# Bias of Exp and Square as a number in the instruction, in a four-layer graph kernel

## The chip, the cores and the metric

The kernel runs on one core of a Trainium2 chip. A core has five engines with a queue of instructions each: PE multiplies matrices into PSUM, DVE and POOL do elementwise work and reductions, ACT evaluates functions such as Exp, Square and Sigmoid, and SP issues DMAs. The engines run beside one another and wait on semaphores. The metric is the device time of one execution in microseconds (us), lower is better.

## The reference

Four graph layers run one after the other on x (4096 nodes, 64 features) with one adjacency matrix (4096 x 4096, zeros and ones). Each is followed by `x = layernorm(x + layer(x))`.

- Layer 0: neighbours' mean (`adj @ x`), a linear layer, relu, row normalization.
- Layers 1 and 3, the hyperbolic attention layers: for every pair of nodes i, j a weight `sigmoid(left_i + right_j + b) * adj_ij` times a curve of the pair's distance, then a sum over j:

```python
adj_att = sigmoid(left[:, None] + right[None, :] + b_att[0]) * adj
x_local = logmap(x[:, None, :], x[None, :, :], c)
support_t = einsum('ij,ijd->id', adj_att, x_local)
return proj(expmap(x, support_t, c), c)
```

- Layer 2: of each row's neighbours the last counts 1, the one before it 1/2, then 1/4 and so on, by a running count of the row's ones:

```python
pos = rank - (deg - k)
w = mask * where(pos > 0, 0.5 ** (k - pos), 0.0)
out = w @ (x @ weight) + bias
```

## The kernel before

The nodes are cut into 32 blocks of 128 (`BLOCKS`, taken from the last to the first) and into 4 groups of 1024 columns (`GROUPS`, also from the last). Each layer passes over all groups, and in each group over 16 loads of adjacency (`load`, L698), 1 MB each and two blocks wide, issued on SP into six buffers. Row work on a finished group (normalizing, the next layer's operands) is written as Python generators, of which `tick` advances a few steps at each block, so that it is issued among the next group's pair work.

**Attention (layers 1 and 3, function `attend`).** For one block j and 1024 columns:
- PE forms `z` in PSUM, three matmuls for each half of 512 columns (L1059 adds the adjacency, L1062 and L1065 the pair's distance). `z` has three buffers.
- ACT makes `sig`, the Sigmoid of `left_b` with a bias column of `right` (L1074). This bias differs by row and stays a pointer.
- ACT makes `sq[:, k]`, the Square of `z` (L1077). Its bias is the tile `turn`, one number in each of 128 partitions, all equal.
- DVE multiplies the cut-off `z` by `sig` into `t[:, k]` (L1080).

After two blocks DVE combines `sq` and `t` in one instruction over 2048 columns (L1082). `sq` has two buffers, `t` and `sig` three. PE sums `t` over the blocks into `acc` (L1037), two pairs of blocks late. There are 128 such pairs, 64 in each attention layer.

**Layer 2 (`wide_pass` for the first two groups together, `narrow_pass` for the third and fourth).** PE adds to a running count in `z` for each block (L1569, function `count`); ACT turns the count into the weight by an Exp (L1576, function `weights_of`), whose bias is the tile `at_edge`, again the same number in all partitions; PE multiplies the weights with `halves` (L1581, `add_up`). The count stays in the same PSUM tile from block to block, so that PE can add the next block only when Exp has read the last one. An Exp reads 1024 columns in the wide pass and 512 in the narrow ones.

**Order.** Layers 0 and 2 are issued under `tc.manual_schedule(engines=FIXED)`, which keeps PE and ACT in the order written. Attention is not: there the framework's scheduler orders each engine's instructions, with row work tied behind pair work by `mark`. DVE and POOL are ordered by the scheduler throughout. A tile that is written and read gets its semaphore waits from the framework.

The two constants are written once at the start:

```python
turn = num(keep, "turn", 1)
V.memset(turn, ROOT + OFF)
at_edge = num(keep, "at_edge", 1)
V.memset(at_edge, -(OFF_EDGE + CUT) * LN2)
```

A copy without a function (`nc.scalar.copy`) also runs on ACT, among others `sums` from `acc` (L1088), `top` and `low` (L1439, L1441), `left_b` (L1021) and the operands of row work (L947). Its casts of `ys` and `yd` are L899 to L901. Row work also has a Square of `u` without bias (L1134), a Tanh without bias (L1164), and Ln with a bias of 1.0 given as a number (L950, L951).

Of the kernel before, what the change touches and what calls it, by code (L numbers as in the profile page):

```python
# [14 lines left out]
AF = mybir.ActivationFunctionType  # L15
# [28 lines left out]
ROOT = 1.3933509672239  # L44
OFF = 0.044942809516658
HIGH = 1.3261200051291
Z_TOP = 0.0655
UNIT = 2.0**16
MEAN_TOP = 1e-10

LN2 = 0.6931471805599453
OFF_EDGE = 255.0
CUT = 27.0
# [5 lines left out]
def gnn_stack_kernel(  # L59
# [15 lines left out]
    nc = tc.nc  # L75
    V = nc.vector
# [11 lines left out]
    for src, at in ((b0, 0), (b2, D), (b_att1, 2 * D), (b_att3, 2 * D + 1), (r1, 2 * D + 2)):  # L88
        n = src.shape[0]
# [22 lines left out]
    def num(pool, name, n=NB):  # L112
        return pool.tile([P, n], F32, name=name)
# [455 lines left out]
    def stream(fits):  # L569

        with ExitStack() as st:

            def pool(name, bufs=1, **kw):
                return st.enter_context(tc.tile_pool(name=name, bufs=bufs, **kw))

            keep = pool("f_keep")
# [37 lines left out]
            def tick(n):  # L614
                for _ in range(n):
                    place[1] += 1
                    mark(False)
                    for queue in queues:
                        while queue and queue[0][1] <= place[1]:
                            wait = next(queue[0][0], None)  # L620
                            if wait is None:
                                queue.pop(0)
                                continue
                            queue[0][1] = place[1] + wait
                            if wait:
                                break
                    mark(True)

            def later(steps, second=False, wait=0):
                queues[second].append([steps, place[1] + wait])  # L630

            def in_turn(tag, *parts):
                for part in parts:
                    yield from (part or ())
                done.add(tag)
# [5 lines left out]
            def need(tag):  # L641
                while tag not in done:
                    assert queues[0] or queues[1], tag
                    tick(1)
# [51 lines left out]
            def load(s, g):  # L696
                a = loads.tile([P, 2, WW], F32, name="edges")
                nc.sync.dma_start(a, adj[s, :, 2 * g : 2 * g + 2, :])  # L698

                return a, a.rearrange("p b i -> p (b i)").bitcast(BF16)[:, 1::2]  # L700
# [79 lines left out]

            two_i = keep.tile([P, P], BF16, name="two_i")
            V.tensor_scalar(two_i, ident, 2.0 * UNIT, None, ALU.mult)
            turn = num(keep, "turn", 1)
            V.memset(turn, ROOT + OFF)


            centre = keep.tile([P, 2, D + 1], F32, name="centre")
# [209 lines left out]
            def in_order(one, behind):  # L997

                tc.add_manual_dep(
                    one, behind.name,  # L1000
                    mybir.DependencyInfo(
                        mybir.DependencyClass.NoSync, mybir.DependencyReason.DATA
                    ),
                    reason="order of issue",
                )

            def spread_left(s):

                left_bs[s] = lefts.tile([P, WW], F32, name="left_b")
                for h in range(2):  # L1010
                    yield from free()
                    t = take(F32, P, W)
                    for k in range(SB):
                        nb = s * WB + h * SB + k
                        nc.tensor.transpose(
                            t[:, k * P : (k + 1) * P],
                            left[:, nb : nb + 1].to_broadcast([P, P]),
                            ident,
                        )
                    yield near()  # L1020
                    nc.scalar.copy(left_bs[s][:, h * W : (h + 1) * W], t)  # L1021
                    held.pop()
                    yield 1

            def attend(layer, s, rate, then):

                left_b = left_bs[s]

                acc = ps.tile([P, W], F32, name="acc")
                lag = []  # L1030

                def add_up(g, t, behind=None):

                    for k in (1, 0):
                        j = 2 * g + k
                        for h in range(2):
                            it = nc.tensor.matmul(  # L1037
                                acc[h * D : (h + 1) * D, :], xe[:, j, :],
                                t[:, k, h * W : (h + 1) * W],
                                start=j == BLOCKS[0], stop=j == BLOCKS[-1],  # L1040
                            )
                            if behind is not None:
                                in_order(it.ins, behind.ins)

                for g in reversed(range(NB // 2)):
                    _, edge = load(s, g)
                    need((layer, 2 * g // WB))
                    if g == 4 and then is not None:
                        later(in_turn((layer, then, "left"), spread_left(then)), True)
                    for k in (1, 0):  # L1050
                        j = 2 * g + k
                        of = slice(j * P, (j + 1) * P)

                        zp = z_tile()
                        for h in range(2):
                            half = zp[:, h * W : (h + 1) * W]
                            to = slice(s * WW + h * W, s * WW + (h + 1) * W)
                            at = k * WW + h * W
                            nc.tensor.matmul(  # L1059
                                half, two_i, edge[:, at : at + W], start=True, stop=False  # L1060
                            )
                            nc.tensor.matmul(  # L1062
                                half, hi_lo[:, of], lo_hi[:, to], start=False, stop=False
                            )
                            last = nc.tensor.matmul(  # L1065
                                half, src[:, of], dst[:, to], start=False, stop=True
                            )
                        if k == 1:
                            if len(lag) == 2:
                                add_up(*lag.pop(0), last)  # L1070
                            sq = sb.tile([P, 2, WW], F32, name="sq")
                            t = sb.tile([P, 2, WW], F32, name="t", bufs=3)
                        sig = sb.tile([P, WW], F32, name="sig", bufs=3)
                        nc.scalar.activation(  # L1074
                            sig, left_b, AF.Sigmoid, bias=right[:, j : j + 1]
                        )
                        nc.scalar.activation(  # L1077
                            sq[:, k], zp, AF.Square, bias=turn, scale=-1.0 / UNIT
                        )
                        V.scalar_tensor_tensor(t[:, k], zp, 0.0, sig, ALU.max, ALU.mult)  # L1080
                        tick(rate)
                    V.scalar_tensor_tensor(t, sq, HIGH**2, t, ALU.add, ALU.mult)  # L1082
                    lag.append((g, t))
                    tick(rate)
                for args in lag:
                    add_up(*args)
                sums = row.tile([P, W], F32, name="sums", bufs=2)
                nc.scalar.copy(sums, acc)  # L1088
                return sums
# [200 lines left out]
            )  # L1290
            V.tensor_sub(enter, enter, edge_of)
            V.tensor_sub(pass_by, pass_by, enter)
            at_edge = num(keep, "at_edge", 1)
            V.memset(at_edge, -(OFF_EDGE + CUT) * LN2)


            w2_twice = keep.tile([P, D], F32, name="w2_twice")
# [157 lines left out]
            def z_tile():  # L1455
                return ps.tile([P, WW], F32, name="z", bufs=3)
# [116 lines left out]

            def weights_of(z, n, w):

                weighed[0] = nc.scalar.activation(w, z[:, :n], AF.Exp, bias=at_edge, scale=-LN2)  # L1576

            def add_up(acc, j, *ws):
                for part in range(2):
# [8 lines left out]
            weighed = [None]  # L1588
# [46 lines left out]
            sq = row.tile([P, D], F32, name="w_sq")  # L1635
# [16 lines left out]

    fits = const.tile([P, 1], F32, name="fits")
    stream(fits)

    n_fit = const.tile([1, 1], I32, name="n_fit")
# [54 lines left out]
```

## Time and profile before

| what | value |
|---|---|
| median of 3 runs | 1103.39 us (1102.56 to 1103.76) |
| profiled execution, its own time | 1103.6 us |
| its span, first to last instruction | 1101.8 us |
| mean granted PE clock | 0.966 |
| busy: PE, DVE, ACT, POOL | 997.7, 916.4, 795.1, 273.5 us |
| L1077, Square of attention | 256 instructions, 277.9 us |
| L1576, Exp of layer 2 | 128 of 512 columns, 81.3 us, and 64 of 1024 columns, 68.0 us |
| L1074, Sigmoid of attention | 256 instructions, 286.0 us |
| attention of layer 1 and of layer 3 | about 195 to 520 us and 750 to 1070 us |
| layer 2 | about 520 to 750 us |

A row of a group of instructions gives line, engine, operation, output<-inputs, shapes and count; after the first bar the busy time in us and the mean duration of one in ns; after the second the engine's idle time just before them, and what ended it. A row of the chain of waits in order of time gives start in us, length in us, and the work: the chain goes back from the last instruction, at each step to what released it or to the instruction before it on its engine. "issue" is time in which the engine waited for nothing that the profile shows, and a name with q is the engine's sequencer. Instructions that follow one another overlap in their records, so starts are a better measure of pace than durations.

### The profile page before, as it was taken

To read this page: it belongs to the slowest core of one execution; us is meant where nothing else is said; L and a number is where in the kernel's file an instruction comes from. 1 tells how busy PE (TensorE), PEld (TensorE's weight loads), DVE (VectorE), ACT (ScalarE), POOL (GpSimd) and SP (SyncE) were. 2 spreads that over 40 slices of the span, in tenths; PEclk is the share of its full clock that TensorE was granted. 3 is DMA by queue.
4 is the path that set the end of the run, shared out by engine and by line. 5 is a ranking of instruction groups with operands and counts; after the bars stand their busy time and mean duration, and the time that the engine had idled before them with its cause. 6 is when DMAs were issued, how large, how long until landed. Compare 5 with 4: busy or idle time off the path is not lost.

```text
span 1101.8 us, 13740 instructions
## 1 busy us (share of the span) xinstructions
PE 997.7 (91%) x4862; PEld 394.3 (36%) x4949; DVE 916.4 (83%) x1452; ACT 795.1 (72%) x886; POOL 273.5 (25%) x649
## 2 busy tenths in 40 slices
PE   4998997889999999998998998998899999999980
PEld 2454454333333333332333333322333333333320
DVE  6677976999999999999457395636999999999986
ACT  0003122979999999897676778989899999998950
POOL 0011210010053533625500010100001544346172
PEclk8999998889999999999998999999999999999995
DMA  9999999536666566655787988776556666666400
GB/s 358 378 411 388 369 421 382 189 122 223 214 244 211 195 234 214 222 198 184 271 304 280 366 298 277 273 261 229 191 192 217 241 228 202 238 222 228 163 1 23
DMA packets 38581, 271.63 MB, mean 247 GB/s; under 512 B 4710, under 2 KB 4710, under 8 KB 5734
## 3 DMA queue, kind: packets, MB, share of 16 engines
q1 hardware_dynamic: 37728, 270.03, 67.4%
q8 instruction: 41, 0.67, 0.2%
q10 hardware_dynamic: 774, 0.63, 0.2%
q14 instruction: 38, 0.31, 0.1%
HBM read 269.58 MB, written 1.05 MB: 246 GB/s over the span
## 4 chain that ended last, share of the span: by engine, by line
PE 56%; DVE 26%; ACT 8%; DMA 3%; POOL 3%; issue 3%; ACTq 0%; SPq 0%; POOLq 0%; DVEq 0%
PE acc L1037 15%; PE z L1569 9%; DVE t L1082 8%; PE z L1062 7%; PE z L1059 7%; PE z L1065 6%; DVE t L1080 6%; PE acc L1581 3%; PE acc L1414 3%; ACT sq L1077 3%; DMA edges<-in_adj_dram 3%; DVE junk L838 2%; ACT sq L1576 2%; PE z L1581 1%; POOL sq L869 1%
## 5 line engine op out<-in xcount | busy, mean ns | idle before, releaser
L1080 DVE SCALAR_TENSOR_TENSOR t<-z,sig 128x1024 f32<-128x1024 f32 x256 | 309.3, 1219 | 13.8 <-ACT sq L1077 7.5
L1077 ACT ACTIVATE sq<-z,turn 128x1024 f32<-128x1024 f32 x256 | 277.9, 1111 | 46.5 <-PE z L1065 19.4
L1082 DVE SCALAR_TENSOR_TENSOR t<-sq,t 128x2048 f32<-128x2048 f32 x128 | 297.4, 2324 | 0.5
L1074 ACT ACTIVATE sig<-left_b,right 128x1024 f32<-128x1024 f32 x256 | 286.0, 1146 | 1.9 <-DVE t L1080 1.3
L1037 PE MATMUL acc<-t,xe 128*64 128x512 f32 x1024 | 258.2, 614 | 16.5 <-DVE t L1082 15.7
L1062 PE MATMUL z<-lo_hi,hi_lo 128*128 128x512 f16 x512 | 195.4, 382 | 3.6 <-issue 0.7
L1065 PE MATMUL z<-dst,src 74*128 74x512 f16 x512 | 196.6, 384 | 0.0
L1059 PE MATMUL z<-edges,two_i 128*128 128x512 bf16 x463 | 183.0, 395 | 6.8 <-DVE t L1080 6.8
L1576 ACT ACTIVATE sq<-z,at_edge 128x512 bf16<-128x512 f32 (+1 forms) x192 | 149.2, 828 | 45.2 <-PE z L1569 41.9
L1037 PEld LDWEIGHTS acc<-t,xe 128*64 128x64 f32 x1024 | 64.3, 137 | 145.6 <-issue 85.1
L838 DVE SCALAR_TENSOR_TENSOR t<-edges 128x2048 bf16<-128x2048 f32 x32 | 73.0, 2288 | 37.0 <-DMA edges<-in_adj_dram 37.0
L1059 PEld LDWEIGHTS <-two_i 128*128 128x128 bf16 x512 | 50.5, 99 | 132.7 <-issue 83.9
L1569 PE MATMUL z<-edges,pass_by 128*128 128x512 bf16 x241 | 86.2, 395 | 11.0 <-ACT sq L1576 10.3
L1414 PE MATMUL acc<-edges,first 128*128 128x512 bf16 x241 | 77.0, 396 | 18.4 <-DMA edges<-in_adj_dram 17.9
L1569 PE MATMUL z<-edges,enter 128*128 128x512 bf16 x240 | 84.0, 393 | 0.5
L1414 PE MATMUL acc<-edges,third 128*65 128x512 bf16 x256 | 80.1, 394 | 0.8 <-issue 0.2
L838 DVE SCALAR_TENSOR_TENSOR junk<-edges 128x2048 bf16<-128x2048 f32 x32 | 73.2, 2286 | 4.8 <-DMA edges<-in_adj_dram 4.6
L1065 PEld LDWEIGHTS <-src 74*128 74x128 f16 x512 | 49.4, 97 | 71.0 <-issue 9.1
L1062 PEld LDWEIGHTS <-hi_lo 128*128 128x128 f16 x512 | 50.6, 99 | 54.9 <-issue 10.0
L1581 PE MATMUL acc<-sq,halves 128*64 128x512 bf16 x384 | 61.0, 395 | 2.4 <-issue 1.4
L869 POOL TENSOR_TENSOR sq<-z 128x512 f32<-128x512 f32 x8 | 14.2, 1777 | 166.5 <-DVE z L868 135.1
L1133 POOL TENSOR_TENSOR w_att<-x,u 128x512 f32<-128x512 f32 x6 | 15.6, 2596 | 142.1 <-ACT u L1128 142.1
(375 smaller groups left out, 938.4 us busy)
## 6 DMA issues: line engine op xcount, KB each, us to landing
edges<-in_adj_dram SPq DMA_DIRECT2D x256, 1024.0 KB, 4.9
x<-in_x_dram SPq DMA_DIRECT2D x4, 256.0 KB
out_dram<-x ACTq DMA_DIRECT2D x2, 256.0 KB
out_dram<-x SPq DMA_DIRECT2D x2, 256.0 KB
w_sb<-in_L_gnn_W_dram ACTq DMA_DIRECT2D x1, 32.0 KB, 5.4
w_twice<-in_L_gnn_weight_dram ACTq DMA_DIRECT2D x2, 16.0 KB, 7.4
given<-in_L_gnn_b_dram ACTq DMA_DIRECT2D x1, 0.2 KB
given<-in_L_gnn_bias_dram ACTq DMA_DIRECT2D x1, 0.2 KB
```

What stands on the lines that cost most here:

```text
L838: V.scalar_tensor_tensor(junk, a, 0.0, a, ALU.not_equal, ALU.not_equal, accum_out=odd[:, n : n + 1])
L1037: it = nc.tensor.matmul(acc[h * D : (h + 1) * D, :], xe[:, j, :], t[:, k, h * W : (h + 1) * W], start=j == BLOCKS[0], stop=j == BLOCKS[-1],)
L1059: nc.tensor.matmul(half, two_i, edge[:, at : at + W], start=True, stop=False)
L1062: nc.tensor.matmul(half, hi_lo[:, of], lo_hi[:, to], start=False, stop=False)
L1065: last = nc.tensor.matmul(half, src[:, of], dst[:, to], start=False, stop=True)
L1074: nc.scalar.activation(sig, left_b, AF.Sigmoid, bias=right[:, j : j + 1])
L1077: nc.scalar.activation(sq[:, k], zp, AF.Square, bias=turn, scale=-1.0 / UNIT)
L1080: V.scalar_tensor_tensor(t[:, k], zp, 0.0, sig, ALU.max, ALU.mult)
L1082: V.scalar_tensor_tensor(t, sq, HIGH**2, t, ALU.add, ALU.mult)
L1414: nc.tensor.matmul(accs[h][:m], lhs[:, j, :], edge[:, at : at + W], start=j == BLOCKS[0], stop=j == BLOCKS[-1],)
L1569: nc.tensor.matmul(z[:, h : h + W], lhs, rhs[:, h : h + W], start=j == BLOCKS[0], stop=True, skip_group_check=True,)
L1576: weighed[0] = nc.scalar.activation(w, z[:, :n], AF.Exp, bias=at_edge, scale=-LN2)
```

## The change

Square in `attend` and Exp in `weights_of` get their bias as a Python number in place of the tiles `turn` and `at_edge`. The two tiles and the memsets that fill them go. Scale, function, operands and results stay as they are, as does Sigmoid's bias.

```diff
-            turn = num(keep, "turn", 1)
-            V.memset(turn, ROOT + OFF)
...
-                            sq[:, k], zp, AF.Square, bias=turn, scale=-1.0 / UNIT
+                            sq[:, k], zp, AF.Square, bias=ROOT + OFF, scale=-1.0 / UNIT
...
-            at_edge = num(keep, "at_edge", 1)
-            V.memset(at_edge, -(OFF_EDGE + CUT) * LN2)
...
-                weighed[0] = nc.scalar.activation(w, z[:, :n], AF.Exp, bias=at_edge, scale=-LN2)
+                weighed[0] = nc.scalar.activation(w, z[:, :n], AF.Exp, bias=-(OFF_EDGE + CUT) * LN2, scale=-LN2)
```

## The prediction

> **What bounds the kernel now.** Three views were read in this order: the page's busy shares and its chain of waits, the groups of instructions kept apart by shape, and the chain in order of time. First the page:
>
> ```profile
> PE 997.7 (91%) x4862; PEld 394.3 (36%) x4949; DVE 916.4 (83%) x1452; ACT 795.1 (72%) x886; POOL 273.5 (25%) x649
> ...
> PE 56%; DVE 26%; ACT 8%; DMA 3%; POOL 3%; issue 3%; ACTq 0%; SPq 0%; POOLq 0%; DVEq 0%
> PE acc L1037 15%; PE z L1569 9%; DVE t L1082 8%; PE z L1062 7%; PE z L1059 7%; PE z L1065 6%; DVE t L1080 6%; PE acc L1581 3%; PE acc L1414 3%; ACT sq L1077 3%; DMA edges<-in_adj_dram 3%; DVE junk L838 2%; ACT sq L1576 2%; PE z L1581 1%; POOL sq L869 1%
> ```
>
> ACT is the third busiest engine, and the two lines that change, L1077 (Square) and L1576 (Exp), hold 3% and 2% of the chain. So the change can only win where they stand in that chain. Followed through in time, the chain holds 26 Squares (28.3 us) and 35 Exps (24.7 us), out of 256 and 192.
>
> Next, why they stand there. The chain near the end of layer 3's attention:
>
> ```profile
> 1050.61 2.21 DVE t L1082
> 1052.82 0.02 issue
> 1052.85 0.02 ACTq L1077
> 1052.86 0.04 issue
> 1052.91 1.12 ACT sq L1077
> 1054.03 0.02 issue
> 1054.05 1.23 DVE t L1080
> 1055.28 2.21 DVE t L1082
> ```
>
> This is a ring. L1082 of one pair of blocks releases a Square (its `sq` has two buffers), the Square releases the second L1080, and the next L1082 follows on DVE. One turn takes 1055.28 - 1050.61 = 4.67 us, of which the Square is 1.12. Elsewhere PE sets the pace; its chain when it never waits:
>
> ```profile
> 872.05 1.87 PE acc L1037 x8
> ...
> 876.67 1.87 PE acc L1037 x8
> ...
> 881.29 1.87 PE acc L1037 x8
> ...
> 885.91 1.87 PE acc L1037 x8
> ```
>
> PE's own work for a pair takes 4.62 us, only 0.05 under the ring. Attention is balanced: a faster Square shortens the ring, and PE is next late by 0.05.
>
> In layer 2, Exp reads a running count that PE may add to only after Exp has read it; in the narrow passes the chain goes from a pair of Exps to PE's next count and back:
>
> ```profile
> 653.88 1.27 ACT sq L1576 x2
> 655.15 0.04 issue
> 655.19 0.61 PE z L1569 x2
> ```
>
> **What one instruction loses.** The groups by shape:
>
> ```profile
> L1077 ACT ACTIVATE sq<-z,turn 128x1024 f32<-128x1024 f32 x256 | 277.9, 1111 | 46.5 <-PE z L1065 19.4 <-DVE t L1082 14.6 <-DVE r_t L754 3.0
> L1576 ACT ACTIVATE sq<-z,at_edge 128x512 bf16<-128x512 f32 x128 | 81.3, 687 | 17.8 <-PE z L1569 17.7
> L1088 ACT COPY sums<-acc 128x512 f32<-128x512 f32 x8 | 4.7, 585 | 11.0 <-PE acc L1037 10.7
> L1134 ACT ACTIVATE sq<-u 128x512 f32<-128x512 f32 x6 | 3.8, 628 | 0.0
> L899 ACT CAST ys<-y 128x512 f16<-128x512 f32 x8 | 4.9, 618 | 39.6 <-DVE y L896 39.6
> ```
>
> Nothing here is the changed instruction itself: an Exp or Square from PSUM with no pointer. The nearest is L1088, a copy from PSUM of the same 512 columns without a bias: 585 against 687 ns, so 102 ns less. A copy is not quite an ACTIVATE: from SBUF the pointerless Square of L1134 takes 628 and the cast of L899 618, 10 more. So the price is 102 - 10 = 92 at the low end, 102 at the high end; I take 95. It does not lie in the streaming part: the 1024-column Exp takes 1110, so 512 columns cost 423 ns and the fixed part is 264. Square then takes about 1016 ns, Exp 592 and 1015. The busy time of ACT falls by 448 x 0.095 = 42.6 us, most of it off the path.
>
> [...] If the pointer's read were what lies under the instruction before, only an instruction after a wait would win; that is the third rival.
>
> **What the change removes, adds and moves.** Two DVE memsets at the start (`turn`, 59 ns, at 1.0 us, and `at_edge`, at 1.5): free, because DVE then waits 2.09 us for x and the chain there is the load of the first edges; without that cover they would cost 0.12 us. No wait or DMA is added, no instruction is moved by hand.
>
> **The sum**, against the profiled execution of 1103.6 us (span 1101.8 and 1.8 around it; 0.2 over the median of 1103.39):
> - Layer 2: 35 Exps in the chain x 0.095 = 3.3 us. Behind each is PE's next count or an ACT copy, which move up with it. If PE's other work is next late at half of them, 1.65.
> - Attention, seven Squares between 801.6 and 820.0 us, in layer 3's first group, where the chain runs on ACT itself through copies, Sigmoids and two table loads (1.28 us each): 7 x 0.095 = 0.67.
> - Attention, the other 19 Squares, nearly all in the ring: it falls from 4.67 to 4.57, under PE's 4.62. Each gives 0.05 if PE has a full pair to do, 0.095 if PE waits then. I take 0.07, between them, since PE has both kinds of pairs: 1.33 (0.95 to 1.8).
> - Attention, pairs that the chain puts on PE but that come in the ring's time: among the 78 acc rows of the chain, 11 steps are 4.65 to 4.70 us. 11 x 0.05 = 0.55.
> Together 5.85, about 5.9 us. The 24 steps at 4.60 to 4.65 give nothing, since PE is the bound there. 1103.6 - 5.9 = 1097.7, and 0.2 less for the median: **1097.5 us**. With all low ends (92 ns, Exps halved, 0.04 per ring Square, nothing from PE's steps) the gain is 3.0; with all high ends (102 ns) 6.8. Own range: 1096.4 to 1100.4.
>
> A measurement of this kernel can tell about 0.2% (2.2 us) from no change: faster means under 1101.2, slower over 1105.6.
>
> **Rivals.**
> 1. *PE is the bound, and ACT's time is idle time.* [...] Here PE is 91% busy and ACT 72%. As a mechanism: PE's 4.62 us follow so closely on the ring that the Squares in it give nothing, and only the seven Squares on ACT's own stretch (0.67) and half of the Exps (1.65) are won: 2.3 us, 1101.1, on the edge of what can be told. For it: the 24 PE steps at 4.62. Against: the ring's Squares and the Exps with which PE's next count has to wait.
> 2. *The number is no number:* the framework stores it in SBUF and passes a pointer all the same. Then 1103.4. Against: Ln with a bias of 1.0 (L951, 8 columns) takes 193 ns and Tanh without one (L1164) 208; the fixed 264 of a pointered Exp is missing there. 1.0 may be special, so it keeps a chance.
> 3. *The overlap hides the pointer.* 13 of the chain's Exps are second of two and 6 of the seven Squares follow ACT work; without these 19, 42 x 0.095 = 4.0 us remain: 1099.4. Against: two Exps in a row take 1.27 us, so the second adds 0.58, while the second of two pointerless PSUM copies (L1439 and L1441, starting 94.66 and 95.14) comes 0.48 after the first. The 0.10 are still there when back to back.
> 4. *Slower: the order of attention changes.* Stages 0 and 2 fix the order on PE and ACT, attention does not, and ACT does not run it in the order written: at 1043 to 1062 us it runs Square, Square, Sigmoid, Sigmoid, at 804 to 816 Sigmoid and Square in turn. If the framework weighs a cheaper Square, it may place both Squares of a turn in the ring, ahead of the second L1080. The second adds its pace, 2.12 - 1.11 = 1.01 now, 0.91 after. The turn is then 5.48 instead of PE's 4.62, +0.87 a pair. 10 of the 128 pairs turn the gain into a loss that can be told; with 14 it is 1097.5 + 12.2 = 1109.7. For it: the order visibly varies, and engines this balanced leave little slack. Against: the edit changes no dependence between blocks.
>
> **How the numbers follow.** Forecast 0.52; a new order that helps, gaining over 8 us, 0.04; rival 1 0.16 (half of it under 1101.2); rival 2 0.05; rival 3 0.04; rival 4 0.19. Faster: 0.52 + 0.04 + 0.08 + 0.04 = 0.68. Same: 0.08 + 0.05 = 0.13. Slower: 0.19. The range 1094 to 1106 takes in the unknown price, rivals 1 to 3 and the mild cases of rival 4; it leaves out most of rival 4 (0.15) and the best orders (0.03).
>
> **What would show it.** Right: L1077 at about 1016 ns, L1576 at 592 and 1015, no `turn` or `at_edge` among their inputs; two Exps in a row at about 1.08 us; turns of the ring at 4.6 us; L1077 and L1576 smaller in the chain; the time before layer 2 (520 us) earlier by 1 to 2 us, layer 2 shorter by about 3. Wrong: 1111 and 687 ns as before (rival 2); the shorter durations with unchanged stages (rival 1); turns of 5.5 us, or another sequence of Square and Sigmoid (rival 4).

## The result, and the profile after

| | median us | runs, lowest to highest |
|---|---|---|
| before | 1103.04 | 6, 1099.21 to 1105.3 |
| after | 1093.83 | 6, 1091.98 to 1095.65 |

The ratio is 0.9918, 95% interval 0.9897 to 0.9940: faster by 9.2 us where 5.9 were forecast. 1093.83 lies 0.2 us under the low end of the range (1094). The profiled execution took 1092.3 us, its span is 1090.5 at a mean granted clock of 0.971. Lines of the kernel after are 2 lower than before, from L1294 on 4 lower.

The page of the kernel after, busy shares and chain:

```profile
PE 998.8 (92%) x4949; PEld 392.1 (36%) x4949; DVE 913.0 (84%) x1450; ACT 756.2 (69%) x886; POOL 267.4 (25%) x649
...
PE 66%; DVE 20%; ACT 6%; DMA 4%; issue 2%; POOL 2%; ACTq 0%; SPq 0%; POOLq 0%; DVEq 0%
```

ACT lost 38.9 us of busy time. Its share of the chain fell from 8% to 6% only; 29 Exps (18.5 us) and 15 Squares (13.1 us) are left in it. The groups by shape:

```profile
L1075 ACT ACTIVATE sq<-z 128x1024 f32<-128x1024 f32 x256 | 254.8, 1022 | 57.7 <-PE z L1063 25.2 <-DVE t L1080 19.8 <-DVE r_t L754 3.5
L1572 ACT ACTIVATE sq<-z 128x512 bf16<-128x512 f32 x128 | 69.9, 600 | 25.6 <-PE z L1565 25.6
L1572 ACT ACTIVATE sq<-z 128x1024 bf16<-128x1024 f32 x64 | 62.2, 1021 | 32.0 <-PE z L1565 29.6 <-DVE t L1080 2.3
```

`turn` and `at_edge` are gone from the inputs. The Square takes 1022 ns (1111 before), the Exps 600 (687) and 1021 (1110): 87 to 89 ns each, where 95 were forecast. The Square's wait for L1080 (L1082 before) grew from 14.6 to 19.8 us. Now the ring near the end of layer 3, in the chain in order of time:

```profile
1046.26 1.23 DVE t L1078
1047.49 2.20 DVE t L1080
1049.68 1.14 DVE t L1078
1050.82 0.01 issue
1050.83 1.23 DVE t L1078
```

A turn takes 1050.83 - 1046.26 = 4.57 us, the forecast figure. The chain names DVE alone, but the Square still closes the ring. The timelines of ACT and DVE show it:

```profile
1049.78 1.02 ACT L1075 ACTIVATE sq<-z 128x1024 f32<-128x1024 f32 x1 [0.56 <-DVE t L1080]
```
```profile
1050.83 1.23 DVE L1078 SCALAR_TENSOR_TENSOR t<-z,sig 128x1024 f32<-128x1024 f32 x1
```

The Square starts 0.10 us after L1080's end and itself ends at 1050.80, and the second L1078 begins 0.03 later. The first L1078 ends at 1050.82, so the chain could name either. Where the second one need not wait, it starts some 0.08 us before the first one's end. Of the 69 turns between 4.40 and 4.72 us in this profile, 64 have the second L1078 start less than 0.06 us behind the end of a Square (53 of 62 in the kernel before). So the Square still sets the turn here, by about 0.1 us; DVE's own turn is 4.46 us, as the run with a third buffer shows below. PE's 4.62 is no floor in this place.

The order on PE, ACT and DVE in attention did change, as rival 4 had it. PE and ACT kept theirs in stages 0 and 2, while DVE's row work moved in layer 2 too; POOL and SP kept theirs throughout. So the time can have come from the shorter instructions, from the new order, or from both.

The stages, from the ends of the copies `sums` in each trace, one for each group (us). Kernels with "old order" have the changes named and run in the order of the kernel before:

| profile of | to the first sums | layer 1, other groups | layer 2 and layer 3's first group | layer 3, other groups | last sums to the end | span |
|---|---|---|---|---|---|---|
| before | 291.2 | 236.4 | 318.4 | 228.6 | 27.2 | 1101.8 |
| after | 286.7 | 232.2 | 314.5 | 226.9 | 30.1 | 1090.5 |
| both numbers, old order | 286.1 | 232.9 | 313.8 | 225.2 | 27.4 | 1085.4 |
| Exps only, old order | 289.7 | 236.4 | 315.1 | 228.6 | 27.1 | 1096.9 |
| Squares only, old order | 288.1 | 233.1 | 317.4 | 225.2 | 27.5 | 1091.4 |
| pointers, new order | 284.0 | 233.8 | 320.7 | 228.6 | 30.2 | 1097.3 |

The first column holds layer 0 and layer 1's first group. It differs by some microseconds between profiles of the same program (291.2 and 289.6 for the kernel before, 286.1, 285.8 and 287.9 for "both numbers, old order"), while what follows repeats within 1 us. Of the 11.3 us between the spans of before and after, 4.5 lie in it. The comparisons below start at the first sums where they go by traces.

### The profile page after: what moved, and what is told of

It is laid out like the page before. It is cut to its first block, busy times and chain, and to the rows that moved or that the text cites. A ratio compares the mean times of both kernels' runs of the same rounds, so it can differ in the third digit from the quotient of the medians.

```text
span 1090.5 us, 13825 instructions
## 1 busy us (share of the span) xinstructions
PE 998.8 (92%) x4949; PEld 392.1 (36%) x4949; DVE 913.0 (84%) x1450; ACT 756.2 (69%) x886; POOL 267.4 (25%) x649
## 3 DMA queue, kind: packets, MB, share of 16 engines
HBM read 269.58 MB, written 1.05 MB: 248 GB/s over the span
## 4 chain that ended last, share of the span: by engine, by line
PE 66%; DVE 20%; ACT 6%; DMA 4%; issue 2%; POOL 2%; ACTq 0%; SPq 0%; POOLq 0%; DVEq 0%
PE acc L1035 17%; PE z L1565 9%; PE z L1057 8%; PE z L1063 7%; PE z L1060 7%; PE acc L1410 7%; DVE t L1080 6%; DVE t L1078 6%; DMA edges<-in_adj_dram 4%; PE acc L1577 4%; ACT sq L1572 2%; ACT sq L1075 1%; PE z L1577 1%; PE aux L941 1%; ACT sig L1072 1%
## 5 line engine op out<-in xcount | busy, mean ns | idle before, releaser
L1078 DVE SCALAR_TENSOR_TENSOR t<-z,sig 128x1024 f32<-128x1024 f32 x256 | 309.8, 1219 | 12.6 <-ACT sq L1075 10.5
L1080 DVE SCALAR_TENSOR_TENSOR t<-sq,t 128x2048 f32<-128x2048 f32 x128 | 295.3, 2307 | 0.2
L1075 ACT ACTIVATE sq<-z 128x1024 f32<-128x1024 f32 x256 | 254.8, 1022 | 57.7 <-PE z L1063 25.2
L1057 PE MATMUL z<-edges,two_i 128*128 128x512 bf16 x512 | 201.4, 393 | 8.6 <-DVE t L1078 8.6
L1572 ACT ACTIVATE sq<-z 128x512 bf16<-128x512 f32 (+1 forms) x192 | 132.1, 740 | 57.5 <-PE z L1565 55.2
L1410 PE MATMUL acc<-edges,first 128*128 128x512 bf16 x256 | 81.2, 399 | 17.9 <-DMA edges<-in_adj_dram 17.8
L1565 PE MATMUL z<-edges,enter 128*128 128x512 bf16 x256 | 89.7, 393 | 0.0
L1131 POOL TENSOR_TENSOR w_att<-x,u 128x512 f32<-128x512 f32 x6 | 12.7, 2122 | 143.6 <-ACT u L1126 143.6
```

Of the source, the lines that this page charges most:

```text
L1057: nc.tensor.matmul(half, two_i, edge[:, at : at + W], start=True, stop=False)
L1075: nc.scalar.activation(sq[:, k], zp, AF.Square, bias=ROOT + OFF, scale=-1.0 / UNIT)
L1410: nc.tensor.matmul(accs[h][:m], lhs[:, j, :], edge[:, at : at + W], start=j == BLOCKS[0], stop=j == BLOCKS[-1],)
L1565: nc.tensor.matmul(z[:, h : h + W], lhs, rhs[:, h : h + W], start=j == BLOCKS[0], stop=True, skip_group_check=True,)
```

## The experiments

An order is forced by a function at the end of the issue. It ties each instruction of PE, ACT, DVE and POOL behind the one ahead of it in a list taken from the other kernel's program:

```diff
+            in_given_order()
...
+                if before is not None:
+                    tc.add_manual_dep(one, before.name, ...)
```

**Price or order.** Four kernels on one chip; the kernel before took 1101.22 us there (23 runs, 1096.37 to 1107.21).

Both numbers, old order: the kernel after, with `ORDER` taken from before.

> Both biases are numbers, and every engine runs its instructions in the order of the kernel before (given by added order-only dependences). Price and order: the shorter Exps and Squares alone win about 6 us, 1097, because 61 of them stand in the chain of before at 88 ns each (5.4) and 11 pairs come in the ring's time; the rest of the 9.2 us is the new order's. Price alone: 1093.8, as the change itself. Order alone: 1103, since ACT's time is idle time.

Measured: 1090.92 us (1087.25 to 1095.39), ratio 0.9905 (0.9873 to 0.9936).

Pointers, new order: the kernel before, with `ORDER` taken from after.

> Both biases are pointers, and every engine runs in the order that the framework chose for the changed kernel. Price and order: 1100, 3 us under the kernel before. Price alone: 1103, the order is worth nothing. Order alone: 1094, the whole gain.

Measured: 1105.19 us (1099.03 to 1107.58), ratio 1.0038 (1.0018 to 1.0058).

Exps only, old order:

```diff
-                weighed[0] = nc.scalar.activation(w, z[:, :n], AF.Exp, bias=at_edge, scale=-LN2)
+                weighed[0] = nc.scalar.activation(w, z[:, :n], AF.Exp, bias=-(OFF_EDGE + CUT) * LN2, scale=-LN2)
```

> Only Exp of layer 2 takes a number, Square keeps its pointer, the order is that of the kernel before. Price and order: 35 Exps of the chain at 87 ns, 3.0 us, 1100. Price alone: more, about 5 us (9.2 x 3.3 / 5.85), 1098. Order alone: 1103.

Measured: 1098.17 us (1096.0 to 1103.58), ratio 0.9964 (0.9943 to 0.9985).

The changed kernel again:

> The changed kernel once more, on the same chip as the three others, as the fourth corner of the square of price and order: 1093.8 by all theories.

Measured: 1092.03 us (1089.05 to 1096.82), ratio 0.9913 (0.9882 to 0.9944).

What follows: the shorter instructions alone, with nothing moved, give the whole gain. The new order by itself costs 0.4%. My theory that part of the gain came from the order falls. The Exps' share lies near the forecast 3.3 us, so the surplus seemed to come with the Squares.

**The Squares, up and down.** Four kernels on another chip, the kernel before at 1102.56 us (17 runs, 1095.58 to 1105.66). Squares only, old order:

```diff
-                            sq[:, k], zp, AF.Square, bias=turn, scale=-1.0 / UNIT
+                            sq[:, k], zp, AF.Square, bias=ROOT + OFF, scale=-1.0 / UNIT
```

> Only the Squares take their bias as a number; the Exps keep the pointer at_edge, and the order on PE, ACT, DVE and POOL is that of the kernel before. Open is where the gain of both numbers together (about 10 us in the order before) comes from. Theory A (the Squares' term of the prediction was too small; the Exps' was right): the Square falls from 1.11 to 1.02 us and the run gains 6 to 8 us against the kernel before, ratio 0.993 to 0.995, most of it in the last groups of each attention layer, nothing in layer 2. Rival B (the prediction's own size for the Squares, 2.5 us, and the rest comes only when Exps and Squares change together): ratio 0.997 to 0.998. Rival C (the difference of the runs so far is layer 0's variation, not the Squares): the time from the first Square to the end is that of the kernel before, less 2.5 us at most.

Measured: 1096.38 us (1093.16 to 1100.77), ratio 0.9958 (0.9940 to 0.9976).

By the trace 7.3 us are won from the first sums to the end (810.6 before, 803.3 here), 0.8 of it in layer 2's wide pass and 0.2 in its narrow passes and the group behind them. The medians differ by 6.2 us; the ratio's interval is 2.6 to 6.6 us. The trace and the medians have theory A's size, but the ratio lies between A's 0.995 and B's 0.997, and its interval reaches into both. Rival C is out: from the first Square to the end 7.8 us are won (906.6 to 898.8). The long turns and stretches below say what the 7.3 are made of. A second pointer:

```diff
+            slope = num(keep, "slope", 1)
+            V.memset(slope, -1.0 / UNIT)
...
-                            sq[:, k], zp, AF.Square, bias=turn, scale=-1.0 / UNIT
+                            sq[:, k], zp, AF.Square, bias=turn, scale=slope
```

> The other way: pointers as in the kernel before, and the Squares' scale is a second pointer, to a tile slope; order of the kernel before. Theory A (the ring of L1082, Square and second L1080 sets the pace in the last groups, so the Square's length counts there at full): if a second pointer costs what the first does, the Square goes from 1.11 to about 1.20 us, the ring from 4.66 to 4.75, and the run loses 6 to 10 us, about what the Squares gain with a number. Rival B (PE's 4.62 covers most of it): a loss of 2 to 4 us. If the second pointer costs nothing, the Square stays at 1.11 us and the time does not change, and the run tells nothing of the ring.

Measured: 1108.94 us (1106.05 to 1111.8), ratio 1.0071 (1.0045 to 1.0097). The Square takes 1204 ns, 93 more than with one pointer, and turns of the ring 4.75 to 4.78 us. The sign follows the dose: 89 ns less wins, 93 ns more loses 6.4 us.

Then the ring itself, with room made in another pool, and first that room alone:

```diff
-            loads = pool("f_loads", 6)
+            loads = pool("f_loads", 5)
```

> A control for the next run: pointers and order as before, but five instead of six buffers in the pool f_loads, which makes room. Both theories: within 3 us of the kernel before, by whatever the loads of layer 2 lose.

Measured: 1118.45 us (1117.19 to 1120.43), ratio 1.0158 (1.0132 to 1.0185). A miss: the sixth load buffer is worth 16 us, about 10 of them ahead of the first sums by the profiles. As a control it still serves.

```diff
-                            sq = sb.tile([P, 2, WW], F32, name="sq")
+                            sq = sb.tile([P, 2, WW], F32, name="sq", bufs=3)
```

> The control, and sq with three buffers in place of two; pointers and order as before. It takes away what makes the Square of a pair wait for the pair's turn of L1082, and leaves the Square at 1.11 us. Theory A (the ring through sq sets the pace in the last groups): the ring opens, pairs there fall from 4.66 towards PE's 4.62 and the steps of 5.5 us shrink, so 3 to 8 us less than the control. Rival (ACT's and DVE's own work is the pace there, not the buffer): within 1.5 us of the control.

Measured: 1111.24 us (1108.66 to 1115.53), ratio 1.0096 (1.0068 to 1.0124), 7.2 us less than the control. With a third buffer the turns fall from 4.66 to between 4.46 and 4.54 us although the Square still takes 1.11. The ring through `sq` is what set the pace there. Layer 2's weights share the tile's name and got the third buffer too, but of the 6.4 us that the profile wins behind the first sums 6.2 lie in attention's other groups of layers 1 and 3.

**Where the surplus lies.** A step of L1082 in the ring goes from 4.66 to 4.57 us, as forecast, and not every step keeps it. What the forecast lacked are single places. The first kind, in the kernel before, is in the timeline of DVE and then of POOL (start, length, both in us):

```profile
1011.73 3.11 DVE L1082 SCALAR_TENSOR_TENSOR t<-sq,t 128x2048 f32<-128x2048 f32 x1
```
```profile
1010.65 1.05 POOL L1214 TENSOR_TENSOR w_att<-x,p 128x512 f32<-128x512 f32 x1
1011.65 1.05 POOL L1215 TENSOR_TENSOR u<-u,q 128x512 f32<-128x512 f32 x1
1012.77 3.11 POOL L1218 TENSOR_TENSOR x<-u,w_att 128x512 f32<-128x512 f32 x1
```

L1082 takes 3.11 us instead of 2.28, and POOL's product L1215, which began 0.08 us ahead of it, ends 0.96 us after L1082's start. Then POOL's next product waits in turn: 3.11 instead of 1.05. With numbers L1082 comes first; the same two products in the kernel after:

```profile
999.21 2.28 DVE L1080 SCALAR_TENSOR_TENSOR t<-sq,t 128x2048 f32<-128x2048 f32 x1
```
```profile
998.22 1.04 POOL L1212 TENSOR_TENSOR w_att<-x,p 128x512 f32<-128x512 f32 x1
999.22 3.17 POOL L1213 TENSOR_TENSOR u<-u,q 128x512 f32<-128x512 f32 x1
```

Now POOL waits, and in this place nobody waits for POOL. In "both numbers, old order" three such turns are gone against before (at 293.9, 460.0 and 1011.7 us), each about 0.9 us.

The second kind is TensorE at half clock. The chain of the kernel before shows what two such stretches cost, one in the last narrow pass of layer 2 and one at the end of layer 3, PE's last eight accumulations taking 3.55 us where eight took 1.87 elsewhere:

```profile
719.72 1.82 PE z L1569 x4
...
1070.38 3.55 PE acc L1037 x8
```

In the kernel after four such `z` take 1.01 us at the same place in layer 2 (711.02).

In the clock records of the kernels before and after, the granted clock is 1.0 or 0.5, and a stretch at 0.5 ahead of the tail lasts 3.41, 6.83 or 10.24 us. In each of the 17 profiles the stretches start on a grid, any two of them a whole number of 3.41 us apart to within 0.02. Two windows of the grid at the end of layer 3 follow, first of the kernel before, then of "Squares only" (start and end, length, busy us of PE, PEld, DVE, ACT and POOL, granted clock, DMA share, GB/s):

```profile
1066.80:1070.21 3.41, 0.79 (x4) 0.00 (x0) 3.31 (x3) 0.00 (x0) 2.96 (x7) 1.00 0.00 0
1070.21:1073.62 3.41, 3.24 (x8) 0.77 (x8) 0.12 (x1) 0.00 (x0) 2.40 (x13) 0.50 0.03 5
```
```profile
1056.01:1059.42 3.41, 1.94 (x8) 0.48 (x8) 3.30 (x5) 0.00 (x0) 2.96 (x14) 1.00 0.00 0
1059.42:1062.84 3.42, 1.49 (x8) 0.48 (x8) 1.87 (x1) 0.00 (x0) 2.94 (x6) 1.00 0.02 5
```

In the kernel before, PE is busy only 0.79 us of the window that ends just ahead of the accumulations (1070.38), and the next window has half the clock. In "Squares only" the accumulations begin at 1061.35; the grid cuts the same idle time in two, PE is busy 1.94 and 1.49 us of the windows, and the clock stays full. In all 13 profiles with the old order PE is busy 1.25 or 1.26 us of the 4 us up to the end of the last L1082. Where a window starts 0.12 to 0.72 us ahead of that end (5 profiles), the accumulations run at half clock; at 1.29 to 1.87 us (6) they run at full clock; at 2.34 and 2.72 us the half clock comes in the midst of them. So in all 13 the clock here went with the grid's place, whatever the instructions cost. The loss in a stretch, the sum of (1 - clock), is 1.7 us (3.41 x 0.5), or 3.4 where two join. From the first to the last sums the kernel before has 6 such units, "Exps only" 6, "Squares only" 3, "both numbers, old order" 3 in two profiles and 4 in one, the kernel after 5. In three places their cost can be read step by step. The last accumulations take 4.1 to 4.2 us from the last L1082 to the sums in profiles of the kernel before and of "Exps only", 2.6 in those with both numbers. The last step of layer 1's fourth group is about 6.3 or 5.5 us, the first only where a stretch lies between 512 and 518 us. And PE's three rounds of `z` and `acc` from 717.54 us in layer 2 end at 723.92, after 6.38 us; in the kernel after three such rounds take 4.77 (707.81 to 712.58), 1.6 less.

Two more runs are to tell chance from program, beside a repeat and a try at the tail (kernel before 1103.53 us, 23 runs, 1097.05 to 1106.99). The kernel before as a run of its own:

> The kernel before, unchanged, as a run of its own: what the comparison can tell. A ratio of 1.000 within 0.002. If the half-clock stretches and the long turns of L1082 belong to the program and not to chance, the profile has them in the same places: L1082 at 3.11 us in the last group of layer 3, the last eight accumulations at 1.06 us, and six stretches of half clock between 290 and 1075 us. If they are chance, their places or number differ.

Measured: 1101.19 us (1096.91 to 1105.23), ratio 0.9987 (0.9965 to 1.0008). Its profile has the same seven long turns of L1082 and the same six units of half clock in the same places. So the long turns belong to the program's timing. For the stretches this run cannot tell, because the grid lay almost alike in both profiles: counted from the first sums, a window starts 0.78 us later in the one and 0.35 in the other. A second pointer for the Exps:

```diff
+            slope = num(keep, "slope", 1)
+            V.memset(slope, -LN2)
...
+                weighed[0] = nc.scalar.activation(w, z[:, :n], AF.Exp, bias=at_edge, scale=slope)
```

> Pointers and order as before, and the Exps' scale is a second pointer too: an Exp of 512 columns goes from 0.69 to 0.78 us. Theory A (35 Exps of the chain at their price): a loss of about 3.3 us, spread over layer 2. Theory B (what the runs so far suggest: the Exps' own share is some 2.5 us, and the rest of the 3.4 us won by shorter Exps was one stretch of half clock of TensorE at 718 us that did not come; such a stretch costs up to 1.7 us): the loss is 2.5 us plus or minus whole stretches, so 1 to 6 us, and it lies in a few places, each with its granted clock at 0.5.

Measured: 1106.31 us (1100.15 to 1112.2), ratio 1.003 (1.0002 to 1.0057); an Exp takes 776 ns. The two narrow passes lose 5.6 us together, more than the 35 Exps of the chain would (3.1). But only two units of half clock are left between the sums, and the last group of layer 3, in which nothing was changed, is 1.6 us shorter: its last accumulations run at full clock. So the stretches do not belong to the long instructions as such. They come or stay away with small shifts of the program against the grid, and which of them come was not forecast by either theory.

The repeat of both numbers in the old order:

> The run with both numbers and the order of the kernel before once more, beside the next one on the same chip. Expected again at 0.988 to 0.993 of the kernel before, with the same three half-clock stretches between 290 and 1058 us.

Measured: 1089.89 us (1087.86 to 1092.46), ratio 0.9896 (0.9871 to 0.9922). Its profile has four units of half clock, not three: 590 to 597 us has two in place of one, and the interval to layer 2's first sums is 0.9 us longer. The program is the same; the grid is not (a window starts 0.76 us after the first sums here, 3.01 and 3.16 in the two other profiles), so this 0.9 is chance. At like places of the grid, this profile against that of the kernel before, there are 4 units in place of 6, and 10.3 us are won from the first sums on (810.6 to 800.3). The tail, DVE's `n` moved in the order list:

```diff
  order of the kernel after, DVE, last group
-  n (L754)   y (L1131)   uu (L1134)   d (L1136)
+  y (L1131)   uu (L1134)   d (L1136)   n (L754)
```

> Both numbers and the order of the changed kernel, but DVE's last n (it waits for POOL's chain of row work) stands behind the last group's own three row steps on DVE instead of ahead of them. Theory (in the new order the last group's rows stand behind that n, which costs the changed kernel some 3 us after the last sums): from the last sums to the end 28 us in place of 30.7, and 2 to 3 us less than the changed kernel in all, so 0.987 to 0.990 of the kernel before. Rival (POOL's chain ends last in any order, so what is won ahead of n is lost behind it): 30.7 us still, and the changed kernel's time.

Measured: 1092.4 us (1089.55 to 1094.66), ratio 0.9911 (0.9883 to 0.9939). A miss: the three row steps moved up, yet the tail is still 28.9 us (30.1 in the kernel after), and the time is that of the kernel after. In the chain DVE's row work now goes on behind `n` (L784 here) with the step after the three:

```profile
1067.48 0.17 DVE n L784
1067.69 0.15 DVE k L769
```

POOL's chain ends here 6 us after the last sums (1061.5), as the rival had it. In the new order POOL starts its `p` (L1182) 4.7 us ahead of the last sums, in "both numbers, old order" 9.5.

**The collision by itself.** One more step on POOL in the kernel before, of 0.2 us, whose output nobody uses; PE, ACT and DVE in the old order (kernel before 1101.51 us, 17 runs, 1097.55 to 1105.76):

```diff
                 yield soon()
+                if G.on_pool:
+                    G.mul(G.nums("pool_t"), q, r)
                 E.tensor_mul(w, xg, over(p))
                 E.tensor_mul(u, u, over(q))
```

> Pointers and order as before, and one more small step on POOL (128x8, about 0.2 us, its output unused) in each of the six groups whose row work POOL does, just ahead of the two row products of 512 columns (w_att, u). Theory (L1082 and a POOL product exclude each other, whoever starts first; in the kernel before the product of L1215 starts 0.08 us ahead of L1082, which waits 0.83 us for it): the extra step puts the product behind L1082, so in the fourth group of each attention layer the turn of L1082 falls from 3.11 to 2.28 us and its step from 5.50 to 4.67, the product takes about 3.2 us in place of 1.05, and these two places are earlier by 0.9 us each: about 1.8 us less than the kernel before in the profile, although work was added; by the times 0.997 to 1.000. Rival (the long turns come from something else, such as the pointer's Squares or PSUM): 3.11 us still, and the time of the kernel before or 0.2 us more.

Measured: 1099.24 us (1094.57 to 1101.48), ratio 0.9974 (0.9957 to 0.9992). The timelines of POOL and DVE:

```profile
1006.72 0.20 POOL L1244 TENSOR_TENSOR pool_t<-q,n 128x8 f32<-128x8 f32 x1
1006.88 3.10 POOL L1246 TENSOR_TENSOR u<-u,q 128x512 f32<-128x512 f32 x1
```
```profile
1006.79 2.28 DVE L1111 SCALAR_TENSOR_TENSOR t<-sq,t 128x2048 f32<-128x2048 f32 x1
```

The product now starts 0.09 us behind L1082 (L1111 here): L1082 is back at 2.28 us with pointers, its step goes from 5.49 to 4.67, and the product takes 3.10. Of the seven long turns (5.2 us over 2.28 in all) three are left (1.9 us). The fourth groups are shorter by 1.5 and 1.2 us and the third ones by 0.6 each, while 1.2 are lost in layer 2's first narrow pass and 1.2 in the tail, so that 1.4 us remain at the end. Work was added and the kernel became faster; this shows the collision and excludes a cause of the long turns on ACT or PE.

The same step in the best kernel so far, beside a control (kernel before 1103.64 us, 11 runs, 1100.58 to 1109.66):

> Both numbers and the order of the kernel before, beside the next run on the same chip. Expected at 0.988 to 0.992 of the kernel before; two turns of L1082 of 3.18 us, in the third groups of both attention layers, as in its earlier profiles.

Measured: 1090.56 us (1089.01 to 1092.51), ratio 0.9887 (0.9867 to 0.9908).

> The same with the extra step of 0.2 us on POOL ahead of its row products. Theory (each long turn of L1082 is a collision with a POOL product that started first): the two turns of 3.18 us in the third groups become 2.28, since the product now starts behind them, which gives up to 0.7 us in each of these groups; in the fourth groups, where L1082 was ahead already, nothing changes unless the shift brings another product ahead of it. From the first sums to the end about 1 us less, so 0.998 to 1.000 of the run beside it. Rival (a shift helps in the kernel before by chance and only moves collisions here): as many long turns as before, in other places, and no gain or a loss of 1 us.

Measured: 1089.54 us (1086.48 to 1092.3), ratio 0.9878 (0.9855 to 0.9901). Both turns of 3.18 us become 2.28, and only two of 2.72 are left. That gives 0.3 us in each third group, the rest is taken back by other steps; from the first sums to the end 798.8 in place of 799.4 us. It is the fastest of all that ran, but its interval and its control's overlap.

## Why the prediction was right in sign and too small

Against "both numbers, old order", from the first sums on, 11.2 us are won (810.6 to 799.4). One profile of each kernel, read group by group:

| | forecast | read in the traces |
|---|---|---|
| layer 2, Exps in the chain | 3.3 | about 2.8 |
| attention, Squares in the chain and PE's steps | 0.67 + 1.33 + 0.55 = 2.55 | about 1.9 |
| long turns of L1082 that are gone, three | none | 2.7 |
| stretches of half clock that do not come, net | none | 3.9 |

The third row is 0.9 + 0.92 + 0.92. The fourth is 1.59 (last accumulations of layer 3), 0.73 (last step of layer 1's fourth group), 1.6 (last narrow pass of layer 2), 0.9 (one stretch less at 598 us), less 0.9 for a new one at 664; the stretch at 598 is the one that the repeat of the same program has again, and the one at the end of layer 3 went with the grid's place in all 13 profiles of the old order, so their 0.9 and 1.59 are chance that shifts of the program bring about, not the price of an instruction. The first is what layer 2's three intervals lost, 4.4, less the 1.6 that half clock makes of it. The second is what is left of attention's groups: 0.4 in each third group, 0.45 and 0.5 in the fourth ones, 0.2 in layer 3's first. The sum is 11.3, the tail gives 0.2 back; that it meets the total says only that nothing large was overlooked, since the rows were taken out of the same intervals.

- *The price, 95 ns:* 87 to 89 by the durations. Two Exps in a row take 1.08 us (1.27 before), so the second wins its 0.09 too, and rival 3 is out, like rival 2.
- *Layer 2:* the 35 Exps were right in size. The rest of what layer 2 won is the stretch of half clock at 718 us.
- *The ring, 4.67 to 4.57:* right to the hundredth. The seven Squares on ACT's own stretch gave about 0.2 instead of 0.67. The floor was named wrongly: in the last groups the ring runs at 4.57 turn after turn, with the Square still in it, and PE's 4.62 takes the gain back only in the middle groups. DVE's own turn of 4.46 would be the next bound there.
- *Rival 1* is out: 9.2 us, not 2.3. Its cause, PE as the bound, is true of the second and third groups of layer 3, which gained 0.0 and 0.4 us.
- *Rival 4:* the reordering came, and it cost less than feared. No turn of 5.48 with two Squares in the ring appeared. The new order costs 4.5 us by the traces from the first sums (803.9 after, 799.4 in the old order), 2.7 of it in the tail; by the times 1.1 us on the same chip, and 0.4% with pointers.
- *The step that failed* is "with all high ends ... 6.8". The sum let a shorter instruction win its own price where it stands in the chain, and no more. It left out that two costs in the trace of before hang on when things start: L1082 at 3.04 us in the chain, where other turns take 2.2, and the chain's 3.55 us for eight accumulations. The two are some 6.6 of the 11.2 us, where the sum had put nothing. A shift of 0.1 us turned a long turn around (L1082 from 3.11 to 2.28 us), and with the grid's place a stretch came or stayed away (1.59 us at the end of layer 3), so they belong in the range on both sides; the low end of 1094 left them out.
- *The change as made* is not explained in full. The new order takes 4.5 of the 11.2 us back, so it won 6.7 from the first sums on (810.6 to 803.9), by itself within the sum's high end. About 2.5 of the 9.2 us (an estimate: 9.2 - 6.7) lie ahead of the first sums, where the sum has 4 of its 26 Squares. No run shows a cause for them, so it is open why the result fell just outside the range and not just inside; as far as is known, that part is chance.

Not settled: the time to the first sums. Seven profiles with both numbers have 284.8 to 288.5 us there, seven with six load buffers, a pointer and the old order 287.6 to 291.2, but "pointers, new order" has 284.0. In all these the first Square starts between 187.5 and 196.6 us, before any changed instruction of the pair work has run, and layer 1's first group takes 94.2 to 97.6 from there, so most of the spread is layer 0's.

## What to carry to other kernels

Before a price is multiplied by a count, go through the chain for instructions that take longer than their group's median and ask what they collided with: here such places and the stretches of half clock made some 6.6 of the 11.2 us, and the sum had put nothing on them. Where one engine's product and another's exclude each other, as L1082 and POOL's did here (3.11 us against 2.28), try a fifth of a microsecond of extra work on the side that nobody waits for: here it made the kernel faster (ratio 0.9974, 0.9957 to 0.9992). Take a stretch of half clock for chance until profiles in which the grid lies differently agree on it. And compare a change with its order held fixed: here the framework moved other work as well, and the new order took back 4.5 us by the traces.

## What the runs showed of the hardware

- DVE's L1082 and POOL's instructions of 512 columns exclude each other wherever they meet in the kernel before; the second waits for the first. In seven turns POOL's started first, and L1082 took 2.72 to 3.30 us in place of 2.28; in five L1082 started first and kept its 2.29, and POOL's took 2.58 to 3.30 (1.18 where it started first). After four of the seven, POOL's next product took 3.11 us in place of 1.05. DVE's excess in each of the seven long turns is the rest of POOL's instruction less 0.13 us (0.83 for a product that ends 0.96 after L1082's start).
- TensorE's granted clock was 0.5 in units of 3.41 us, each a loss of 1.7 us of clock. The stretches lie on a grid of 3.41 us in each of the 17 profiles, and its place against the first sums differs between profiles of the same program (3.01, 0.76 and 3.16 us).
- PE's busy share in the window ahead went with the clock. From the first to the last sums of the kernel before, PE was busy 23 to 48% of the five windows at full clock that were followed by one at half clock, and at least 52% of each of the 218 that were followed by one at full clock; in the kernel after, 27 to 34% of four and at least 56% of each of 216. The 17 profiles together are less clear-cut: 68 windows at full clock were followed by one at half clock, and PE was busy at most 51% of each. 3730 were followed by one at full clock; PE was busy under 50% in 11 of them, and under 43% in none.
- A second pointer cost like the first: 93 ns on the Square (1204 against 1111), 89 and 90 on the Exps (776 against 687, 1200 against 1110), where the first cost 89, 87 and 89.
